# Weights of the first blocks and normalised tokens issued by ScalarE, list scatters spaced anew, in a cross-attention and mixture-of-experts kernel

## The chip, the cores and the metric

The kernel runs on one core of one Trainium2 chip. The metric is the device time of one launch in microseconds (us). An engine is named by its role: TensorE (PE, matrix products; PEld are its weight loads), VectorE (DVE), ScalarE (ACT), GpSimd (POOL) and SyncE (SP), which only starts DMAs. ScalarE and SyncE have a hardware DMA queue each; GpSimd starts the indirect DMAs (gathers and scatters), whose rows are picked by indices.

## The reference

Four batches of 1024 tokens of width 256 pass a cross-attention with 16 heads over 77 context rows, and then a layer of 9 experts of which each token uses 2. Cut to what matters:

```python
x = x + xattn(ctx, layernorm(x), ...)      # 16 heads, 77 keys for each batch
xf = layernorm(x)                          # (4096, 256)
probs = softmax(xf @ Wr)                   # 9 experts
topk_w, topk_idx = top_k(probs, 2)
cw = scatter(topk_w / sum(topk_w))         # (4096, 9), two entries in a row
gate = silu(einsum('th,ehi->tei', xf, Wg)) # 256 -> 704
hidden = gate * einsum('th,ehi->tei', xf, Wu)
x = x + einsum('tei,eih,te->th', hidden, Wd, cw)
```

## The kernel before

**Two halves.** The first half is the attention. It works on 32 sub-blocks of 128 tokens, 4 of which make a group (8 groups, `NS = 4`, `NG = 8`). The second half is the experts. A token's two (expert, token, weight) entries are written into a list in DRAM, `list_d`, which has a stretch for every expert. Blocks of 128 or 256 places of that list are then worked one after another: a gather of the entries (`ids`), a gather of the normalised tokens (`yin`, from `y_d` in DRAM), a turn (`px`, `xT`), the products with Wg and Wu (`hidden_pair`, tiles `pg`, `sl`, `hid`), the product with Wd (`down`, tiles `po`, `co`), and a scattered add into the output (`adding`).

**The order is written out by hand.** Each engine runs its instructions in the order in which the Python code emits them, and a queue's DMAs go out in that order, too. An instruction that waits holds up all that stand behind it on its engine.

**The attention loop** (lines 1667 to 1765) runs 33 steps. Step i does for sub-block i the scores in three parts (`scores`, L295, TensorE, then the row maximum on VectorE; `exponentials`, L312, ScalarE). For sub-block i - 1 it scales the attention weights (`attention_weights`, L334), turns them in blocks of 32 on VectorE (`weights_turn`, L352) and sends them to DRAM as `a_d`; `weights_back` (L360) reads them back as `aT` in four DMAs, with the parts in the other order. For sub-block i - 3 (`LAG = 3`) it multiplies `aT` with the values (`values`, L372, tile `po`). The tile `anT`, from which `a_d` is written, exists once, so the next turn on VectorE waits until `a_d` has been read out. TensorE's order in a step is: the three parts of the scores, then the values. The values of sub-block 29 come in step 32, behind the turn of block 0's tokens; those of sub-blocks 30 and 31 come inside block 0, behind its first and its fourth chunk (`in_first`, L1788).

**Routing**, once for each group, is spread over the steps: `residual`, `root`, `logits`, `exponential`, `normalised` (L977: ScalarE makes the normalised tokens `y`, four activations, and SP writes them to `y_d`), `choices`, `ranks`, `places`. `places` puts eight scatters of the group on the list `pending`; `scatter` (L1065) sends one of them, behind an instruction that is named to it, so that they go out one by one.

For groups 0 to 5 the write of `y` is put off to the end of the step (`written`, L1756), behind `weights_back`; for groups 6 and 7 it is issued at once.

**Early blocks.** Blocks 0 to 5 (`EARLY = 6`) hold places that are known to be full from groups 0 to 3 alone (`G_EARLY = 4`), so their gathers wait for the 32 scatters of these groups only. `next_place` (L1647) is called twice in a step. It sends a scatter, or, once the 32 are out and `first_fetch` (L1658) has run (end of step 26), the next of the first gathers. `first_fetch` also prepares the weights of blocks 0 and 1 in parts: `load` (L1360) is a generator with three parts (one DMA for Wg, three for Wu, two for Wd) in front of which the expert's number is read into a register of the issuing engine. One part goes out at the end of a step (L1752), so block 0's weights go in steps 27, 28 and 29; what is left, block 1's weights, goes out behind the loop (L1766).

**Blocks.** `hidden_pair` (L1437) makes a block's hidden rows in six chunks of columns. After each chunk come `pump` (L1574), which emits up to 12 steps of the work that is left over (routing of groups 6 and 7, then the tables of the later blocks), and in blocks 0 and 2 to 5 some scatters: four behind each of chunks 1 to 4 of block 0, two behind each of chunks 0 to 4 of blocks 2 to 5. When the late tables reach a marked point (`PLACES`), `pump` sends all that is pending. `fetch` (L1597) runs at the head of each block and starts weights, gathers of entries (`tokens`) and gathers of tokens (`inputs`) some blocks ahead. The gather of block 6's entries waits for all 64 scatters; `tokens` (L1388) sends what is still pending in front of it.

Of the kernel before, what the change touches and what calls it, by code (L numbers as in the profile page):

```python
# [15 lines left out]
P = 128  # L16
# [5 lines left out]
def kernel(  # L22
# [18 lines left out]
    nc = tc.nc  # L41
# [6 lines left out]
    E, _, FF = wg.shape  # L48
# [4 lines left out]
    NS = TB // P  # L53
    NG = TOK // TB
    GPB = N // TB
    NF = FF // P
    FT = FF - NF * P
# [43 lines left out]
    G_EARLY = NG - 4  # L101
# [193 lines left out]
    def scores(i, k):  # L295

        h, n = banks[k]
        if k == 0:
            nmx[i] = stat.tile([P, H], F32, tag="mx", name=f"mx{i}")
        psc = pscs[k] = ps_sc.tile([P, TB], F32, tag=f"sc{k}", name=f"psc{i}_{k}")  # L300
        w = n * J + (E if h + n == H else 0)
        for c in range(C):
            strips(
                psc[:, :w], turned_query(i, c), g_sb[i // NS // GPB][:, c, h * J : h * J + w],
                start=(c == 0), stop=(c == C - 1),
            )
        return nc.vector.tensor_reduce(  # L307
            nmx[i][:, h : h + n], psc[:, : n * J].rearrange("p (h j) -> p h j", h=n), AX.X,
            ALU.max, negate=True,
        )  # L310
# [597 lines left out]
    for b in range(B):  # L908
        for m in range(2):
            at = 2 * b + m  # L910
# [66 lines left out]
    def normalised(g):  # L977

        y = pools["rpool"].tile([P, NS, D], F32, tag="y", name=f"y{g}", bufs=1)
        r = routed[g]["r"]  # L980
        o = off_mean("fo", g, routed[g]["mv"], r)
        for s in range(NS):
            yield nc.scalar.activation(
                y[:, s, :], xg[g][:, s, :], AF.Identity,
                bias=o[:, s : s + 1], scale=r[:, s : s + 1],
            )
        written.append(
            lambda: nc.sync.dma_start(out=y_d.rearrange("(g p s) d -> g p s d", p=P, s=NS)[g], in_=y)
        )
        if g > NG - 3:  # L990
            written.pop()()
# [73 lines left out]
    def scatter(behind=None):  # L1065

        if not pending:
            return
        place_i, entry, s = pending.pop(0)
        i = nc.gpsimd.indirect_dma_start(  # L1070
            out=list_d[:, :],
            out_offset=bass.IndirectOffsetOnAxis(ap=place_i[:, s : s + 1], axis=0),
            in_=entry.bitcast(I32)[:, s, :], in_offset=None,
            bounds_check=E * LP - 1, oob_is_err=False,
        )
        if behind is not None:
            after(i, [behind], "the lists' places go out one by one")

        apart(i, sent, "other places of the lists")
        apart(i, early_got, "an early block's places are those of earlier groups")  # L1080
        sent.append(i)
# [242 lines left out]
    def weights(j, in_parts=False):  # L1324

        _, i, kind = blocks[j]
        if kind == "quad2":
            wgus[j], downs[j] = quads.pop(i)
            return
        if j == LAST:  # L1330
            w, d = late["w", uppers[j][0]], late["d", uppers[j][0]]
        else:
            w = pools["wpool"].tile([P, C, 2 * FF], F32, tag="wgu", name=f"wgu{j}")
            d = of(wds, next_down[0])
            next_down[0] += 1
        more = uppers.get(j, ()) if j < LAST else ()
        wgus[j] = (w, *(late["w", n] for n in more))
        downs[j] = (d, *(late["d", n] for n in more))
        if kind == "quad":
            quads[i] = wgus[j], downs[j]  # L1340
        at = PARTS[kind] * i
        parts = load(tabs[kind][0][0:1, at : at + 1], w, d)
        if in_parts:
            partly.append(parts)
        else:
            advance(parts)
# [10 lines left out]

        return begin

    def load(number, w, d):  # L1360
        e = nc.values_load(number, engines=[mybir.EngineType.SP], min_val=0, max_val=E - 1)
        wg_v = wg.rearrange("e (c p) f -> e p c f", p=P)[bass.ds(e, 1)].rearrange("o p c f -> (o p) c f")
        wu_v = wu.rearrange("e (c p) f -> e p c f", p=P)[bass.ds(e, 1)].rearrange("o p c f -> (o p) c f")


        nc.sync.dma_start(out=w[:, :, 0:FF], in_=wg_v)
        yield True
        nc.sync.dma_start(out=w[:, :, FF : FF + FT], in_=wu_v[:, :, NF * P :])
        nc.sync.dma_start(out=w[:, :, FF + FT : FF + FB], in_=wu_v[:, :, FA : NF * P])
        nc.sync.dma_start(out=w[:, :, FF + FB :], in_=wu_v[:, :, 0:FA])  # L1370
        yield True
        nc.sync.dma_start(
            out=d[:, 0:NF, :],
            in_=wd[bass.ds(e, 1), 0 : NF * P, :].rearrange("o (f p) d -> p (o f) d", p=P),
        )
        nc.sync.dma_start(
            out=d[64:128, NF, :], in_=wd[bass.ds(e, 1), NF * P : FF, :].rearrange("o p d -> (o p) d")
        )
        yield True
# [57 lines left out]
    def hidden_pair(j, also={}, upcoming=iter(())):  # L1437

        (w,), xT, hid = wgus.pop(j), xTs.pop(j), hids[j % 2]
        for f in range(NF + 1):  # L1440
            pg = mm_tile(f"pg{j}_{f}").rearrange("p (g t) -> p g t", g=2)
            for g, at in enumerate((f * P, UP[f]) if f < NF else (f * P,)):
                for c in range(C):
                    nc.tensor.matmul(  # L1444
                        pg[:, g, :], w[:, c, at : at + P], xT[:, c, :],
                        start=(c == 0), stop=(c == C - 1),
                    )
            sl = pools["spool"].tile([P, TS], F32, tag="sl", name=f"sl{j}_{f}")
            if f < NF:
                nc.scalar.activation(sl, pg[:, 0, :], AF.Silu)  # L1450
                made = nc.vector.tensor_tensor(hid[:, f, :], pg[:, 1, :], sl, ALU.mult)  # L1451
                for _ in range((0, 4)[f > 0] if not j else 2 if j > 1 else 0):
                    scatter(made)
            else:
                nc.scalar.activation(sl[64:128, :], pg[0:64, 0, :], AF.Silu)
                nc.vector.tensor_tensor(
                    hid[64:128, NF, :], pg[64:128, 0, :], sl[64:128, :], ALU.mult
                )
            pump()
            advance(upcoming, 3)  # L1460
            for fn in also.get(f, ()):
                fn()
# [111 lines left out]
    def pump():  # L1574

        if held[0]:
            held[0] -= 1
            return
        for _ in range(STEP if rest else 0):
            got = next(rest[0], None)  # L1580
            if got is None:
                rest.pop(0)
                if not rest:
                    fetch()
                return
            if got is PRODUCT:
                held[0] = HOLD
                return
            if got is PLACES:
                while pending:  # L1590
                    scatter()
                return

    UPPER = [(f"upper{k}", weights_upper(k), LEAD + k) for k in range(1, SETS + 1)]
# [2 lines left out]
    def fetch():  # L1597

        end = known()
        lead_y = LEAD_Y if late else LEAD  # L1600
        for name, fn, lead in (
            ("weights", weights, LEAD), *(UPPER if late else ()),
            ("inputs", inputs, lead_y), ("tokens", tokens, lead_y + 2),
        ):
            if name == "inputs":

                while ahead["tokens"] < min(now[0] + lead_y + 1, end):
                    advance(tokens(ahead["tokens"]))
                    ahead["tokens"] += 1
            while ahead[name] < min(now[0] + lead + 1, end):  # L1610
                got = fn(ahead[name])
                if name in ("inputs", "tokens"):
                    advance(got)
                ahead[name] += 1
# [32 lines left out]
    def next_place(behind):  # L1647

        if first_gathers and len(sent) >= 2 * NS * G_EARLY:
            got = next(first_gathers[0], None)  # L1650
            if got is None:
                first_gathers.pop(0)
                return next_place(behind)
            after(got, [behind], "gathers go out one by one")
        else:
            scatter(behind)
# [10 lines left out]
    for i in range(N_SUB + 1):  # L1667
# [33 lines left out]
            ranks(q - 1)  # L1701
        if now_on:
            if i:
                scores(i, 2)
                exponentials(i, 2)
                queries_logits(i)
            if i + 2 < RIDE:
                query(i + 2)
            if RIDE <= i + FAR < N_SUB:
                query(i + FAR)  # L1710
            if i:
                extra(i, 2)
            if i == END:
                vsides.close()
        else:
            turn(0)
# [136 lines left out]
```

## Time and profile before

| what | value |
|---|---|
| median of 11 runs | 847.27 us (846.0 to 853.17) |
| the profiled execution, time / span | 847.53 us / 845.8 us |
| mean granted TensorE clock | 0.998 |
| attention loop, TensorE's last scores | end at about 320 us |
| block 0's first product to the last product | 332.88 to 837.98 us |
| VectorE, ScalarE, GpSimd busy | 68%, 44%, 36% |
| SP's queue | 166.96 MB, 62.4% of the 16 DMA engines |
| ScalarE's queue | 70 packets, under 0.01 MB |

The span runs from the first to the last instruction. In an order of time, a row gives the start in us, the duration in us, the engine, the line, the operation and its tiles, and in square brackets how long the engine had stood idle before and what released it. `SPq` rows are the issues of SP's DMAs, not the transfers. The list of waits gives, for an engine and what it waited for, the total in us, how often, and the longest. A table by stretches of time gives each engine's busy time and the busy share of the DMA engines (1.0 is all 16 busy).

Around the end of the loop the DMA engines are busy as follows (share, GB/s), by that table: 288 to 292 us 1.05, 353; 296 to 300 us 1.09, 254; 304 to 308 us 0.85, 201; 308 to 312 us 1.04, 366; 320 to 324 us 0.37, 129; 336 to 340 us 0.49, 161; 344 to 348 us 1.06, 370.

### The profile page before, as it was taken

The numbers are of one execution on the slowest core, as the hardware profiler recorded it, in microseconds if no ns is written. First come the engines' busy times: TensorE is split into PE (matmuls) and PEld (weight loads), VectorE is DVE, ScalarE is ACT, GpSimd is POOL, SyncE is SP. The second block draws the span as 40 slices with busy tenths as digits, with TensorE's granted clock in tenths as the row PEclk, the third lists the DMA queues.
The fourth block names the chain that finished last, engine by engine and source line by source line (L and its number), as shares of the span: only waits on it lengthen the run. The fifth ranks groups of instructions, "written<-read, shape, count | busy, mean of one in ns | idle before, by whom it ended". The sixth has DMA issues, their size and how long they took to land. (4 is left out here: it accounts for less than half of the span.)

```text
span 845.8 us, 20860 instructions
## 1 busy us (share of the span) xinstructions
PE 831.3 (98%) x7334; PEld 581.4 (69%) x7334; DVE 579.0 (68%) x1887; ACT 374.4 (44%) x1543; POOL 307.1 (36%) x344
## 2 busy tenths in 40 slices
PE   8999999999999997999999999999999999999996
PEld 6634444445554454788889788788778878877895
DVE  5767779898899986445854585584677566667550
ACT  4778787878878876142222222222222222222221
POOL 3100000123331232577654444544444463453522
PEclk9999999999999999999999999999999999999999
DMA  8028768778578797986785799789779888788421
GB/s 294 5 100 229 207 211 234 226 232 255 180 229 248 218 281 220 330 258 172 206 243 133 207 334 350 188 259 307 209 230 348 265 243 278 209 245 256 115 26 19
DMA packets 129448, 186.04 MB, mean 220 GB/s; under 512 B 26167, under 2 KB 95295, under 8 KB 129216
## 3 DMA queue, kind: packets, MB, share of 16 engines
q1 hardware_dynamic: 111930, 166.96, 62.4%
q0 software_dynamic: 17344, 17.75, 11.8%
q8 instruction: 58, 0.95, 0.5%
q14 instruction: 46, 0.38, 0.1%
q10 hardware_dynamic: 70, 0.00, 0.0%
HBM read 141.08 MB, written 45.00 MB: 220 GB/s over the span
## 5 line engine op out<-in xcount | busy, mean ns | idle before, releaser
L1444 PE MATMUL pg<-xT,wgu 128*128 128x256 f32 x1100 | 243.1, 380 | 0.1
L1444 PEld LDWEIGHTS pg<-xT,wgu 128*128 128x128 f32 x1100 | 208.3, 190 | 30.1 <-issue 1.3
L1560 POOL DMA_INDIRECT out_dram<-co,ids x73 | 116.7, 1599 | 206.6 <-ACT co L1542 131.2
L318 ACT ACTIVATE ex<-psc,mx 128x77 f32<-128x77 f32 x512 | 158.8, 330 | 60.9 <-DVE mx L307 58.5
L1539 PE MATMUL po<-wd,hid 128*128 128x256 f32 (+2 forms) x768 | 173.2, 380 | 0.0
L1539 PEld LDWEIGHTS po<-wd,hid 128*128 128x128 f32 (+2 forms) x768 | 138.7, 183 | 28.6 <-issue 6.2
L143 PE MATMUL po<-u,aT 128*32 128x265 f32 x2560 | 149.5, 387 | 4.4 <-DMA aT<-a_d 4.4
L1417 DVE STREAM_TRANSPOSE xT<-yin 32x128 f32<-32x128 f32 (+1 forms) x528 | 144.7, 274 | 9.0
L1070 POOL DMA_INDIRECT list_d<-line,r_pli x64 | 63.3, 989 | 240.0 <-DVE mx L307 160.5
L1451 DVE TENSOR_TENSOR hid<-pg,sl 128x256 f32<-128x256 f32 x130 | 55.0, 424 | 119.5 <-ACT sl L1450 116.7
L143 PEld LDWEIGHTS po<-u,aT 128*32 128x32 f32 x2560 | 84.6, 110 | 65.8 <-issue 2.9
L1450 ACT ACTIVATE sl<-pg 128x256 f32<-128x256 f32 x130 | 49.8, 384 | 179.0 <-PE pg L1444 169.5
L143 PE MATMUL psc<-g,aT 128*32 128x462 f32 (+1 forms) x1296 | 118.3, 510 | 0.0
L318 ACT ACTIVATION_READ_ACCUMULATOR ex<-psc,mx 128x1 f32 x512 | 107.5, 210 | 0.0
L143 PEld LDWEIGHTS psc<-g,aT 128*32 128x32 f32 x1296 | 42.2, 109 | 64.3 <-issue 51.0
L1542 ACT ACTIVATE co<-po,ids 128x256 f32<-128x256 f32 x66 | 31.2, 474 | 124.6 <-PE po L1539 120.5
L1383 POOL DMA_INDIRECT yin<-y_d,ids x66 | 69.2, 1049 | 34.8 <-issue 17.4
L307 DVE TENSOR_REDUCE mx<-psc 128x6 f32<-128x462 f32 (+1 forms) x96 | 54.3, 565 | 21.6 <-PE psc L143 21.5
L356 DVE STREAM_TRANSPOSE anT<-an 128x1536 f32<-128x1536 f32 x32 | 56.6, 1770 | 4.6 <-DMA a_d<-anT 4.3
L1529 DVE STREAM_TRANSPOSE hid<-hs 32x160 f32<-32x160 f32 (+1 forms) x112 | 39.5, 353 | 1.7
L340 DVE TENSOR_TENSOR an<-ex,rs 128x1024 f32<-128x1024 f32 x32 | 39.2, 1226 | 1.1
L1472 PEld LDWEIGHTS pt<-xT,wgu 128*128 128x128 f32 x308 | 35.1, 192 | 2.1 <-issue 2.0
(378 smaller groups left out, 764.8 us busy)
## 6 DMA issues: line engine op xcount, KB each, us to landing
a_d<-anT SPq DMA_DIRECT2D x32, 768.0 KB
aT<-a_d SPq DMA_DIRECT2D x128, 192.0 KB
wgu<-in_L_ffn_Wg_dram SPq DMA_DIRECT2D x33, 704.0 KB
wd<-in_L_ffn_Wd_dram SPq DMA_DIRECT2D x33, 640.0 KB
wgu<-in_L_ffn_Wu_dram SPq DMA_DIRECT2D x33, 512.0 KB
w_up<-in_L_ffn_Wg_dram SPq DMA_DIRECT2D x12, 704.0 KB
d_up<-in_L_ffn_Wd_dram SPq DMA_DIRECT2D x12, 640.0 KB
w_up<-in_L_ffn_Wu_dram SPq DMA_DIRECT2D x12, 512.0 KB
```

The lines of the kernel that those rows point to most:

```text
L143: nc.tensor.matmul(out[a : a + Q], left(a), right, **kw)
L307: return nc.vector.tensor_reduce(nmx[i][:, h : h + n], psc[:, : n * J].rearrange("p (h j) -> p h j", h=n), AX.X, ALU.max, negate=True,)
L318: nc.scalar.activation(exs[i][:, h + q, :], pscs[k][:, q * J : (q + 1) * J], AF.Exp, bias=nmx[i][:, h + q : h + q + 1], accum_out=sms[i][: ...
L356: made = nc.vector.transpose(turned, an_of[0].rearrange("p (k q t) -> p q k t", q=NQ, t=Q))
L1070: i = nc.gpsimd.indirect_dma_start(out=list_d[:, :], out_offset=bass.IndirectOffsetOnAxis(ap=place_i[:, s : s + 1], axis=0), in_=entry.bit ...
L1383: return nc.gpsimd.indirect_dma_start(out=dst, out_offset=None, in_=src, in_offset=bass.IndirectOffsetOnAxis(ap=offsets, axis=0), **kw,)
L1417: yield nc.vector.transpose(xT[q : q + Q].rearrange("p c (h t) -> p h c t", t=P)[:, :nh, :, a : a + Q], of(yins, j)[a : a + Q].rearrange(" ...
L1444: nc.tensor.matmul(pg[:, g, :], w[:, c, at : at + P], xT[:, c, :], start=(c == 0), stop=(c == C - 1),)
L1450: nc.scalar.activation(sl, pg[:, 0, :], AF.Silu)
L1451: made = nc.vector.tensor_tensor(hid[:, f, :], pg[:, 1, :], sl, ALU.mult)
L1539: nc.tensor.matmul(po[rows, :D], hid[:, f, at], d[:, f, :], start=(f == 0), stop=(f == NF))
L1560: i = nc.gpsimd.indirect_dma_start(out=out_r, out_offset=bass.IndirectOffsetOnAxis(ap=ids[j][:, h, word : word + 1], axis=0), in_=cos[j][: ...
```

## The change

It has four parts.

1. `normalised` issues the write of `y` on ScalarE's queue in place of SP's, for all eight groups, at the same places of the program.
2. `load` takes the queue as an argument. The weights that go out in parts, those of blocks 0 and 1, are issued on ScalarE's queue, and the expert's number is read into ScalarE's register. All other weights stay on SP.
3. From step 24 on, `next_place` is called a third time in each step, behind the third part of the scores.
4. In the blocks, one scatter goes out behind each of the six chunks of blocks 0 to 3, in place of the four and two of before, and the marked point in `pump` sends nothing any more. So that the gather of block 6's entries (and with it the flush in front of it) doesn't come before that, `fetch` holds `tokens` to the early blocks until block 4.

```diff
@@ normalised
-            lambda: nc.sync.dma_start(out=y_d.rearrange("(g p s) d -> g p s d", p=P, s=NS)[g], in_=y)
+            lambda: nc.scalar.dma_start(out=y_d.rearrange("(g p s) d -> g p s d", p=P, s=NS)[g], in_=y)
@@ weights
-        parts = load(tabs[kind][0][0:1, at : at + 1], w, d)
+        parts = load(tabs[kind][0][0:1, at : at + 1], w, d, nc.scalar if in_parts else nc.sync)
@@ load
-    def load(number, w, d):
-        e = nc.values_load(number, engines=[mybir.EngineType.SP], min_val=0, max_val=E - 1)
+    def load(number, w, d, queue=nc.sync):
+        e = nc.values_load(number, engines=[queue.engine], min_val=0, max_val=E - 1)
...
-        nc.sync.dma_start(out=w[:, :, 0:FF], in_=wg_v)
+        queue.dma_start(out=w[:, :, 0:FF], in_=wg_v)
         yield True
-        nc.sync.dma_start(out=w[:, :, FF : FF + FT], in_=wu_v[:, :, NF * P :])
-        nc.sync.dma_start(out=w[:, :, FF + FT : FF + FB], in_=wu_v[:, :, FA : NF * P])
-        nc.sync.dma_start(out=w[:, :, FF + FB :], in_=wu_v[:, :, 0:FA])
+        queue.dma_start(out=w[:, :, FF : FF + FT], in_=wu_v[:, :, NF * P :])
+        queue.dma_start(out=w[:, :, FF + FT : FF + FB], in_=wu_v[:, :, FA : NF * P])
+        queue.dma_start(out=w[:, :, FF + FB :], in_=wu_v[:, :, 0:FA])
         yield True
...
@@ hidden_pair
                 made = nc.vector.tensor_tensor(hid[:, f, :], pg[:, 1, :], sl, ALU.mult)
-                for _ in range((0, 4)[f > 0] if not j else 2 if j > 1 else 0):
-                    scatter(made)
             else:
                 nc.scalar.activation(sl[64:128, :], pg[0:64, 0, :], AF.Silu)
-                nc.vector.tensor_tensor(
+                made = nc.vector.tensor_tensor(
                     hid[64:128, NF, :], pg[64:128, 0, :], sl[64:128, :], ALU.mult
                 )
+            if j < EARLY - 2:
+                scatter(made)
@@ pump
             if got is PLACES:
-                while pending:
-                    scatter()
                 return
@@ fetch
+            if name == "tokens" and now[0] < EARLY - 2:
+                end = min(end, EARLY)
             while ahead[name] < min(now[0] + lead + 1, end):
@@ attention loop
-                scores(i, 2)
+                third = scores(i, 2)
+                if i >= (G_EARLY + 2) * NS:
+                    next_place(third)
```

More of the change, by code (lines that the diff above doesn't have):

```diff
@@ L1358, in weights_upper @@
         return begin
-    def load(number, w, d):
-        e = nc.values_load(number, engines=[mybir.EngineType.SP], min_val=0, max_val=E - 1)
+    def load(number, w, d, queue=nc.sync):
+        e = nc.values_load(number, engines=[queue.engine], min_val=0, max_val=E - 1)
         wg_v = wg.rearrange("e (c p) f -> e p c f", p=P)[bass.ds(e, 1)].rearrange("o p c f -> (o p) c f")
         wu_v = wu.rearrange("e (c p) f -> e p c f", p=P)[bass.ds(e, 1)].rearrange("o p c f -> (o p) c f")
-        nc.sync.dma_start(out=w[:, :, 0:FF], in_=wg_v)
+        queue.dma_start(out=w[:, :, 0:FF], in_=wg_v)
         yield True
-        nc.sync.dma_start(out=w[:, :, FF : FF + FT], in_=wu_v[:, :, NF * P :])
-        nc.sync.dma_start(out=w[:, :, FF + FT : FF + FB], in_=wu_v[:, :, FA : NF * P])
-        nc.sync.dma_start(out=w[:, :, FF + FB :], in_=wu_v[:, :, 0:FA])
+        queue.dma_start(out=w[:, :, FF : FF + FT], in_=wu_v[:, :, NF * P :])
+        queue.dma_start(out=w[:, :, FF + FT : FF + FB], in_=wu_v[:, :, FA : NF * P])
+        queue.dma_start(out=w[:, :, FF + FB :], in_=wu_v[:, :, 0:FA])
         yield True
-        nc.sync.dma_start(
+        queue.dma_start(
             out=d[:, 0:NF, :],
@@ L1375, in load @@
         )
-        nc.sync.dma_start(
+        queue.dma_start(
             out=d[64:128, NF, :], in_=wd[bass.ds(e, 1), NF * P : FF, :].rearrange("o p d -> (o p) d")
```

## The prediction

> **What bounds the kernel now.** I read the page's busy times first, then TensorE's waits, then TensorE and the SP queue in order of time around the places where TensorE stands still.
>
> ```profile
> PE 831.3 (98%) x7334; PEld 581.4 (69%) x7334; DVE 579.0 (68%) x1887; ACT 374.4 (44%) x1543; POOL 307.1 (36%) x344
> PE po L143 <- DMA aT<-a_d: 4.4, 3, 2.4
> ```
>
> TensorE (PE) is busy for 831.3 of 845.8 us, so a change can only gain what lies in the other 14.5 us. In order of time, 7.8 us of these follow its last matmul (it ends at 837.98 of 845.8: scaling, scattered adds), about 2 us are at the start, 0.15 us is at 370, and 4.4 us are three waits for `aT`, the turned attention weights that go out to DRAM (`a_d`) and come back. The change touches neither end. **Its whole possible gain is these 4.4 us**, 0.52%.
>
> ```profile
> 320.57 4.69 PE L143 MATMUL po<-u,aT 128*32 128x265 f32 x80 [0.56 <-DMA aT<-a_d]
> ...
> 328.27 4.69 PE L143 MATMUL po<-u,aT 128*32 128x265 f32 x80 [2.42 <-DMA aT<-a_d]
> ...
> 336.29 4.69 PE L143 MATMUL po<-u,aT 128*32 128x265 f32 x80 [1.42 <-DMA aT<-a_d]
> 340.91 5.45 PE L1444 MATMUL pg<-xT,wgu 128*128 128x256 f32 x24
> 346.29 4.69 PE L143 MATMUL po<-u,aT 128*32 128x265 f32 x80
> ```
>
> The `po` rows are the value products of sub-blocks 28 to 31 (the last one sits inside block 0). The first three waited 0.56, 2.42 and 1.42 us; the fourth, at 346.29, did not. Why aT is late is seen on the SP queue:
>
> ```profile
> 284.61 2.60 SPq L366 DMA_DIRECT2D aT<-a_d  x4
> ...
> 290.67 0.42 SPq L1366 DMA_DIRECT2D wgu<-in_L_ffn_Wg_dram  x1
> 292.36 1.75 SPq L366 DMA_DIRECT2D aT<-a_d  x4
> 296.04 0.34 SPq L357 DMA_DIRECT2D a_d<-anT  x1
> 296.59 1.26 SPq L1368 DMA_DIRECT2D wgu<-in_L_ffn_Wu_dram  x1
> ...
> 303.10 2.61 SPq L366 DMA_DIRECT2D aT<-a_d  x4
> ...
> 330.08 2.09 SPq L366 DMA_DIRECT2D aT<-a_d  x4
> 332.33 0.34 SPq L357 DMA_DIRECT2D a_d<-anT  x1
> 337.86 1.73 SPq L366 DMA_DIRECT2D aT<-a_d  x4
> ...
> 342.36 0.40 SPq L1366 DMA_DIRECT2D wgu<-in_L_ffn_Wg_dram  x1
> ```
>
> Each `aT x4` is issued when the `a_d` before it has landed, so the distance from one aT to the next is one turn of the chain. Before the first weights it was 7.75 us (284.61 to 292.36). Then `wgu` of block 0 goes into the same queue: 10.74 us (to 303.10), 10.09 (to 313.19), 9.42 (to 322.61). Then, with nothing else in the queue, 7.47 (to 330.08) and 7.78 (to 337.86). TensorE takes some 8.9 us for a sub-block, 4.36 of scores and 4.67 of values with a small overlap. The three long turns lose 10.74 + 10.09 + 9.42 - 3 x 8.9 = 3.6 us against it; the last two can't win that back, because behind the loop's last scores TensorE asks for aT sooner (4.69 + 1.99 = 6.7 us after po(29) began).
>
> **The change part by part.**
>
> *Weights of block 0 leave the SP queue* (one issue in step 27, three in step 28, two in step 29). Their bytes stay: 704 + 704 + 704 KB. Off the queue they no longer stand ahead of aT, but they share the DMA engines with it, and these are full there: 1.05, 1.00 and 1.09 busy from 288 to 300 and 1.04, 0.92 and 0.98 from 308 to 320, with a gap only from 300 to 308 (0.83, 0.85). So the order changes more than the sum. Bounds for the start of the last aT, aT(31), now 337.86: nothing gained, 337.9; or three turns at 8.9, or the limit that VectorE sets, which turns weights 30 only behind the maximum of the last scores, at 320.06 + 0.62 = 320.7, and two turns of 7.5 from there: 335.7. I take 337.3, near the upper end, since the engines are full: the weights of step 27 also start 3 us later than now (ScalarE is busy back to back until 293.4) and so meet a_d(27) and aT(27) rather than aT(26).
>
> The Trainium skill, "DMA: Bandwidth & Descriptors", section "Issuing engines are not separate DMA queues", speaks against any gain: queues of different engines run on the same 16 DMA engines, and a second issuer saves issue time only. By that rule aT gains nothing and the sum below would be 847.7. Its section "Queues, rings and completion order" says that a DMA engine goes round the queues it has work for, packet by packet, which would let aT pass the weights and make the sum 844.3; no row here shows two full hardware queues side by side.
>
> *ScalarE issues instead.* The trace shows no such DMA on it but three tiny ones at the start (0.52, 0.22, 0.27 us). From SP's rows: the read of the expert's number took 1.07 us at 289.0 and 1.29 at 340.6 (0.27 on repeats), register work 0.2, an issue 0.37 to 0.43 at a pitch of 0.57. Step 27: 1.07 + 0.2 + 0.1 + 0.42 = 1.8 us. Step 28: 3 x 0.57 + 0.43 for y = 2.1. ScalarE has waits of only 0.32 + 0.33 us there, so the exponentials of sub-block 29 end 3.9 - 0.65 = 3.3 us later, at 310.1 in place of 306.8. TensorE wants that bank for scores(30, 2) at 306.87 + 2 x 1.45 = 309.8: a new wait of 0.3 us, between none (if issuing overlaps the queued activations) and 1.5 (if Wu's first issue takes 1.26 as on SP). All of it lies in front of the 0.56 us wait, which it shortens: nothing. Were that wait gone, it would cost the 0.3.
>
> *y.* Groups 0 to 4 cost ScalarE 0.43 us each, hidden by its distance to TensorE (step 25's exponentials end at 271.5, the next scores need the last bank at about 275). Group 6's is taken together with the next point. Group 7's is not hidden:
>
> ```profile
> 363.76 1.28 ACT L1450 ACT_TABLE_LOAD   x1
> 365.05 0.66 ACT L1450 ACTIVATE sl<-pg 128x256 f32<-128x256 f32 x2
> ...
> 369.37 0.59 ACT L1433 COPY xT<-px 128x512 f32<-128x512 f32 x1
> ```
>
> ScalarE finishes y(7) at 363.74, loads its table, and the two `sl` behind it are already late; xT of block 2 (369.37) ends 0.05 us before TensorE starts block 2 at 370.01, after standing still for 0.15. An issue of 0.34 to 0.43 us plus its hand-over, say **0.45**, goes through to TensorE in full; bounds 0 and 0.6.
>
> *Weights of block 1 move forward.* Now SP issues all six from 342.36, behind aT(31). From ScalarE they follow y(6), which ends at 335.2: y(6)'s write, 1.3 + 0.2 for the number, six issues at 0.57 make 335.2 to 340.6. On ScalarE that delays only block 0's first `sl` (336.5 now); its bank is wanted again at 346.29, so it is hidden with 4 us to spare. On the DMA side it isn't: 2112 KB of weights and 512 KB of y meet aT(31). Undisturbed, aT takes from issue to its product 7.38, 5.66 and 6.21 us (the three waits), so now aT(31) is there at 343.5 to 345.3, and 346.29 covers it by 1.0 to 2.8 us. 768 KB of aT take 2.1 to 3.5 us by themselves (366 and 227 GB/s, the rates of 308 to 312 and 328 to 338); sharing half the engines adds as much again. Bounds: 0 (the weights fit into 336 to 340, where DMA is 0.49 busy) and 3.5 (half rate all through; even wholly behind the 2.1 MB of weights it would be 2.16/0.369 = 5.9). I take 2.6.
>
> **The sum** is read at po(31), where all three waits, new and old, are paid: 337.3 + 5.7 + 2.6 = 345.6 instead of 346.29, -0.7; +0.45 for y(7): **-0.25 us**. The waits of 0.56 and most of 2.42 go; some 1.5 before po(30) stays, because chain and products are both short there; a new wait of about 2 us stands before po(31). Profile: 845.8 - 0.25 span, 847.53 - 0.25 = 847.3 as a run. The median of the runs shown is 847.27, 0.26 below the profiled one: 847.0.
>
> *Scatters and gathers.* GpSimd's work is not on the path. With three in a sub-block, group 3's eight places are out in step 26, not 27, and the first gathers start one step sooner; their tokens, now issued from 303.61, are first used at 325.19 (`px`), so that gains nothing. The list's tail decides when block 6's places can be read: now the last scatter ends at 404.3, the read is at 409.13, the tokens are issued until 414.6, and `px` of block 6 is at 425.65. Later: 9 + 8 + 8 = 25 pending places, at most 24 go out behind chunks, 1 to 3 remain for the flush in front of that same read, at 1.29 each, behind block 2's adds. That is -1 to +3 us, so tokens by 417.6 + 4.7 (median landing) = 422.3: 3 us of cover. Past that each us would stop TensorE at block 6. The rule that holds tokens of block 6 back until block 4 changes nothing: they go out in block 4 now, too. SP has no compute behind it; without y and weights its next wait is block 2's weights, needed 20 us later.
>
> **Rivals.**
> 1. *The weights of block 1 crowd out aT(31)* (slower). One mechanism, at 336 to 346. If nothing was gained before (issue 337.9), aT needs 7.4 as aT(28) did beside the weights, and half rate adds 3.5: 348.8, +2.5; with 0.45 to 0.6 more: **+3.1, 850.4**. It is slower by over 0.3% once aT(31) is ready after 348.4 (346.29 + 2.54 - 0.45). For it: full DMA engines, and that 2.6 MB now come before the last turn, not behind it. Against: half-empty DMA from 336 to 340.
> 2. *The chain comes free* (faster). Two queues let aT pass. Then aT(31) goes at 335.7 and, if the weights don't touch it, is there at 341.4, while TensorE without any wait comes at 346.29 - 4.4 = 341.9. Of these 4.4, VectorE's date for weights 30 leaves a wait: 320.7 + 7.5 + 5.7 = 333.9 for po(30), where TensorE comes at 336.29 - 4.4 = 331.9, less what the chain gains if a_d(30) needn't queue behind aT(29), 0.5 to 2.0; I take 1.0. So -4.4 + 1.0 + 0.45: **-3.0, 844.3**. For it: turns of 7.5 to 7.8 as soon as the queue is clear. Against: DMA busy 1.0.
> 3. *Nothing but the issuer changes*: all waits stay, y(7) adds 0.45: **847.7**. It lies within the forecast's own range.
>
> **How the numbers follow.** A measurement tells about 0.3%, 2.5 us, from no change; the runs shown lie mostly between 846.0 and 849.2. Forecast with rival 3: 0.53. Rival 2: 0.24. Rival 1, with ScalarE's issues costing more than SP's: 0.23. The likeliest case spans 845.4 to 848.4 by itself; with both others taken in until a tenth is left on each side, 844.3 to 849.9.
>
> **What would show it.** Right: aT(29) waits under 1 us, a wait before po(31) of 1 to 3 us, the waits for aT summing to 3 to 4.5 us, 0.4 more before block 2, SP's turns from 292 to 322 at 9 to 10 us. Rival 2: the sum of aT waits under 1.5 us. Rival 1: a wait before po(31) over 4 us. The forecast is wrong in kind if TensorE waits for ScalarE's exponentials by more than 1.5 us around 310, or for block 6's tokens at all.

## The result, and the profile after

The changed kernel takes **858.16 us** (median of 8 runs, 857.04 to 859.97); the kernel before, run beside it, 847.12 us (31 runs). The ratio is 1.013, its 95% interval 1.0117 to 1.0143: about 11 us slower, where the prediction had 847.0 us and a range that ended at 849.9. The profiled execution has a span of 857.2 us, 11.4 more than before.

First the head of the page of the changed kernel: span, TensorE's busy time, and the clock that TensorE was granted, in tenths, in 40 slices.

```profile
span 857.2 us, 20881 instructions
PE 835.3 (97%) x7334; PEld 594.3 (69%) x7334; DVE 578.1 (67%) x1887; ACT 373.3 (44%) x1543; POOL 306.1 (36%) x344
PEclk9999999999999999899999999999999999999998
```

TensorE is busy for 835.3 us where it was 831.3. It has the same 7334 products, so 4 us of the loss are products that run longer; the rest is waiting. Its waits (us in total, times, longest) name one cause, as before:

```profile
PE po L143 <- DMA aT<-a_d: 11.7, 5, 7.1
```

11.7 in place of 4.4. In order of time (start, duration, ..., wait in front of it and what ended it), the value products of sub-blocks 27 to 31 of the changed kernel:

```profile
311.81 4.69 PE L143 MATMUL po<-u,aT 128*32 128x265 f32 x80 [0.57 <-DMA aT<-a_d]
...
321.94 4.69 PE L143 MATMUL po<-u,aT 128*32 128x265 f32 x80 [0.97 <-DMA aT<-a_d]
...
330.14 6.05 PE L143 MATMUL po<-u,aT 128*32 128x265 f32 x80 [2.93 <-DMA aT<-a_d]
...
338.27 4.69 PE L143 MATMUL po<-u,aT 128*32 128x265 f32 x80 [0.15 <-DMA aT<-a_d]
342.88 5.45 PE L1444 MATMUL pg<-xT,wgu 128*128 128x256 f32 x24
355.39 7.06 PE L143 MATMUL po<-u,aT 128*32 128x265 f32 x80 [7.06 <-DMA aT<-a_d]
```

Two things are to be seen. The first four waits sum to 4.6 us, as much as the 4.4 before: nothing was won there. And po(31), which did not wait before, waits 7.06 us. The durations show the rest: po(29) and po(31) take 6.05 and 7.06 us where all others take 4.69. In the windows of 2 us around po(31) (busy time, products, granted clock, DMA share, GB/s) the clock stands at half:

```profile
350.00:352.00 2.00, 0.00 (x0) 1.00 1.11 231
352.00:354.00 2.00, 0.00 (x0) 0.86 1.06 290
354.00:356.00 2.00, 0.60 (x8) 0.50 0.71 257
356.00:358.00 2.00, 2.00 (x24) 0.50 0.96 206
...
360.00:362.00 2.00, 2.00 (x39) 0.93 0.98 338
```

**The sum of the loss:** waits 11.7 - 4.4 = 7.3; slow products (6.05 - 4.69) + (7.06 - 4.69) = 3.7; together 11.0 of the 11.4 us of span.

Why aT(31) comes late shows on the two issuing queues and in the DMA traffic. SP's queue in the changed kernel:

```profile
298.86 0.34 SPq L357 DMA_DIRECT2D a_d<-anT  x1
305.15 2.54 SPq L366 DMA_DIRECT2D aT<-a_d  x4
...
332.52 1.73 SPq L366 DMA_DIRECT2D aT<-a_d  x4
334.41 0.34 SPq L357 DMA_DIRECT2D a_d<-anT  x1
341.40 4.84 SPq L366 DMA_DIRECT2D aT<-a_d  x4
```

aT(31) is issued at 341.40 (before: 337.86), and its four issues are stretched over 4.84 us. The list of SP's waits from 333 to 350 us says what two of them waited for:

```profile
SPq L366 <- DMA y_d<-y: 6.6, 1, 6.6
SPq L366 <- DMA wgu<-in_L_ffn_Wu_dram: 2.4, 1, 2.4
```

In the same stretch of the kernel before, aT's issues wait for nothing but a_d:

```profile
SPq L366 <- DMA a_d<-anT: 5.1, 1, 5.1
```

By the semaphore updates in the changed kernel's trace, a_d(31) had landed at 339.96 and the write of y(6) at 341.32. So the first issue of aT(31) waited 1.4 us longer than its own data asked, for y(6), and the third waited 2.4 us for a part of block 1's Wu. aT reads neither of the two; the wait is for a completion semaphore that they hold, which is explained below with the run e18. On ScalarE, y(6) and then block 1's weights go out just ahead of it:

```profile
335.57 2.06 ACT L983 ACTIVATE y<-x,fo,r_r 128x256 f32<-128x256 f32 x4
337.66 0.34 ACTq L988 DMA_DIRECT2D y_d<-y  x1
338.81 0.39 ACTq L1366 DMA_DIRECT2D wgu<-in_L_ffn_Wg_dram  x1
...
341.03 0.38 ACTq L1372 DMA_DIRECT2D wd<-in_L_ffn_Wd_dram  x1
345.25 0.53 ACTq L1376 DMA_DIRECT2D wd<-in_L_ffn_Wd_dram  x1
345.81 1.28 ACT L1450 ACT_TABLE_LOAD   x1 [8.18 <-DMA wgu<-in_L_ffn_Wu_dram]
```

The last issue comes 3.8 us behind the fifth, and ScalarE computes nothing for 8.18 us, from the end of y to its table load; that will matter below. The DMA queues (packets, MB, share of the 16 engines; q10 is ScalarE's, q1 SP's) from 341.5 to 344.9, when two quarters of aT(31) had been issued:

```profile
q10 hardware_dynamic: 893, 1.04, 90.9%
q8 instruction: 1, 0.02, 1.7%
```

and from 345 to 354:

```profile
q1 hardware_dynamic: 769, 1.44, 65.9%
q10 hardware_dynamic: 813, 0.86, 42.9%
```

For 3.4 us SP's queue moves no packet. The first one of aT(31) starts at 345.0, 3.6 us behind its issue; in the kernel before it is 0.9 us. So aT(31) does not share with the weights that were issued ahead of it at first, it stands behind them. Then it shares with their rest, with `out_dram` and with block 2's Wg.

### The profile page after: what moved, and what is told of

Its sections match the earlier page's. It is cut to its first block, busy times and chain, and to the rows that moved or that the text cites. A ratio compares the mean times of both kernels' runs of the same rounds, so it can differ in the third digit from the quotient of the medians.

```text
span 857.2 us, 20881 instructions
## 1 busy us (share of the span) xinstructions
PE 835.3 (97%) x7334; PEld 594.3 (69%) x7334; DVE 578.1 (67%) x1887; ACT 373.3 (44%) x1543; POOL 306.1 (36%) x344
## 5 line engine op out<-in xcount | busy, mean ns | idle before, releaser
L143 PE MATMUL po<-u,aT 128*32 128x265 f32 x2560 | 153.6, 394 | 11.7 <-DMA aT<-a_d 11.7
L143 PEld LDWEIGHTS po<-u,aT 128*32 128x32 f32 x2560 | 93.1, 111 | 68.6 <-DVE bn_f L393 7.4
L143 PEld LDWEIGHTS psc<-g,aT 128*32 128x32 f32 x1296 | 46.5, 109 | 60.2 <-issue 48.9
```

The source lines that it names most:

```text
L143: nc.tensor.matmul(out[a : a + Q], left(a), right, **kw)
```

## The experiments

The main theory before the runs, **place**: what costs is that block 1's 2.1 MB stand ahead of aT(31). Its rivals: **chain** (block 0's issues on ScalarE make the chain of a_d and aT late), **issuer** (issues hold up ScalarE), **scatter** (the list's new places).

Chips turned out to differ: the kernel before took 847 us on the chips of the first four runs and of the last two, and 870 to 872 us on three others. So ratios are compared within a group, and waits with care.

**The parts undone one by one (847 us).** In the call of the loader and in the write of y, by turns:

```diff
-        parts = load(..., nc.scalar if in_parts else nc.sync)
+        parts = load(..., nc.scalar if in_parts and j == 0 else nc.sync)   # e1
+        parts = load(..., w, d)                                            # e2, e4
-            lambda: nc.scalar.dma_start(out=y_d..., in_=y)
+            lambda: nc.sync.dma_start(out=y_d..., in_=y)                   # e3, e4
```

Block 1's weights back on SyncE:

> The changed kernel with one thing undone: block 1's weights are issued by SyncE again, block 0's stay on ScalarE. Place theory: block 1's first 2.1 MB stand in front of aT(31), and that is what the changed kernel pays; with them behind, the 7.06 us wait before po(31) and the 2.37 us that po(31) took above 4.69 are gone, 9.4 us together: 848 to 850 us. The other waits (0.57, 0.97, 2.93) and the slow po(29) stay. Chain theory: the loss comes from block 0's issues on ScalarE, which make a_d(27) wait for aT(26) and push the chain 2 to 3.5 us back: no more than half comes back, above 853 us. Scatter theory: nothing comes back, 857 to 859 us.

All weights back on SyncE:

> The changed kernel with both blocks' weights on SyncE, so that the last y blocks from ScalarE and the new places of scatters and tokens are what is left. Place theory and chain theory alike: no weights ahead of aT(31), a_d(27) no longer behind aT(26), the waits of the kernel before (4.4 us) return: 846.5 to 848.5 us. Scatter theory: 857 to 859 us. If the y blocks on ScalarE cost something of their own, the time lies over that of the run with y on SyncE too.

y back on SyncE, weights on ScalarE:

> The changed kernel with the last y blocks issued by SyncE again, weights of blocks 0 and 1 still on ScalarE. Place theory: block 1's weights still go ahead of aT(31): 855 to 858.5 us, with a wait before po(31) of 5 us or more. ScalarE theory (the y issues hold up its activations, or the chain): 848 to 853 us.

y and all weights on SyncE, only scatters, gathers and tokens as changed:

> Only the new places of list scatters, of gathers and of normalised tokens; y blocks and all weights on SyncE as before. Place theory: the last scatter is 15 us later than before but nothing waits for it, so 846.5 to 848 us, no change. Scatter theory: 855 us or more.

| kernel | weights 0 / 1 / y from | median us | ratio to before (95%) | wait before po(31) |
|---|---|---|---|---|
| changed | ACT / ACT / ACT | 858.16 | 1.013 (1.0117 to 1.0143) | 7.06 |
| e3 | ACT / ACT / SP | 855.14 | 1.0087 (1.0071 to 1.0104) | 3.26 |
| e1 | ACT / SP / ACT | 849.37 | 1.0035 (1.0023 to 1.0048) | none |
| e2 | SP / SP / ACT | 848.45 | 1.0028 (1.0012 to 1.0044) | none |
| e4 | SP / SP / SP | 848.48 | 1.0027 (1.0016 to 1.0039) | none |

From the changed kernel to e1 the ratio falls by 0.0095, 8 us: moving **block 1's weights** to ScalarE is nearly the whole loss. TensorE in e1 no longer waits at po(31), and the products run at 4.69:

```profile
337.93 4.69 PE L143 MATMUL po<-u,aT 128*32 128x265 f32 x80 [2.04 <-DMA aT<-a_d]
342.55 5.45 PE L1444 MATMUL pg<-xT,wgu 128*128 128x256 f32 x24
347.93 4.69 PE L143 MATMUL po<-u,aT 128*32 128x265 f32 x80
```

e2 against e4: y from ScalarE costs nothing that can be measured by itself. e3: with block 1's weights on ScalarE too, it does. y(6)'s 512 KB then stand in the same queue just ahead of the weights; without them the wait before po(31) is 3.26 instead of 7.06 us and the median 3 us lower. (e3's profiled execution is its slowest, 859.15 us: TensorE waits 3.1 us for a first weight near the start, which the profiles of e1, e2 and e4 don't have. Its waits before po(31) can be read all the same.) What ends aT(31)'s wait on SP's queue in e3 is a weight:

```profile
SPq L366 <- DMA wgu<-in_L_ffn_Wg_dram: 7.4, 1, 7.4
```

a_d(31) lands at 344.70 there, block 1's Wg at 348.31, and aT(31) goes out at 348.38: 3.6 us of waiting for a semaphore that Wg holds, about as long as TensorE then waits. e1 against e2: block 0's weights on ScalarE may cost 0.9 us; the intervals overlap. e4: the scatters' new places cost 0.27%, 2.3 us, where none was expected, and the profile does not show it (its profiled execution, the fastest of seven, has a span of 845.3 us). The scatter theory as the main cause falls; this small part of it stays open.

**Where block 1's weights stand, still from ScalarE.** e13 issues only Wg (704 KB) behind the loop and the rest behind the fifth chunk of block 0; e5 issues all six there.

```diff
     for parts in partly:
-        advance(parts)
+        advance(parts, 1)          # e13 only; e5 drops the loop
-    in_first = {..., 4: [lambda: turn(1)]}
+    in_first = {..., 4: [lambda: [advance(parts) for parts in partly], lambda: turn(1)]}
```

> The changed kernel with block 1's weights still on ScalarE, but issued behind the fifth chunk of block 0 instead of behind the loop. Place theory: it is the order against aT(31) that costs, not the issuer, so the wait before po(31) goes as in the run with block 1's weights on SyncE: 848 to 850 us, the waits before po(28) to po(30) stay at about 4.5 us. If the issuer counts (six issues between ScalarE's activations inside block 0): above 852 us, with gaps of TensorE inside blocks 0 and 1.

> The changed kernel once more, as the measure for the three runs beside it: the last four runs fell on a chip where the kernel before takes 869.85 us instead of 847, with TensorE waiting for xT in blocks 1 to 3, so they can't be set beside the first four. Where the kernel before takes about 847 us: 856 to 860 us, wait before po(31) 6 us or more. Where it takes about 870 us, the wait for aT(31) lies beside a stall that is there anyway: no more than 5 us slower than the kernel before.

> Block 1's weights still from ScalarE, but behind the fifth chunk of block 0. Place theory: no wait of more than 1 us before po(31) and 8 to 10 us less than the changed kernel on the same chip, where the kernel before takes about 847 us. If the issuer counts, no more than 4 us less.

> The changed kernel with only block 1's Wg (704 KB) issued ahead of aT(31) from ScalarE, its Wu and Wd behind the fifth chunk of block 0. aT(31) then shares no completion semaphore with block 1's weights. If the bytes ahead cost (transfers start in the order of issue over both queues): the 1.4 MB that are gone from the front take 3.8 us at 0.37 MB per us, so the wait before po(31) falls from 7.06 to about 3 us, 851 to 854 us where the kernel before takes 847. If the shared semaphores cost: no wait before po(31), 848 to 850 us. If the issuer costs: 856 us or more.

> Block 1's weights from ScalarE, behind the fifth chunk of block 0 (on the two chips where the kernel before takes 870 us this was no different from it). Where the kernel before takes 847 us, place theory: no wait over 1 us before po(31), 848 to 851 us; block 2's weights now stand ahead of block 1's, so a wait of block 1's first products for weights may cost 1 to 2 us of this. If the issuer counts: above 853 us.

> Only block 1's Wg ahead of aT(31), once more and with more rounds: before, on a chip where the kernel before takes 872 us, the wait before po(31) was 1.05 us and the time 867.5 us, ratio 0.9946 with 0.998 as its upper end. Place theory: the same wait of about 1 us on any chip; where the kernel before takes 847 us that is 849 to 851 us, no gain, since what the other chips gain lies in their own stall behind po(31). If the gain holds on another such chip: ratio 0.993 to 0.998 again; if it was chance: 0.999 or more.

> All of block 1's weights behind the fifth chunk of block 0, beside it. No wait before po(31) in any case. Where the kernel before takes 847 us: 848 to 851 us. Where it takes about 870 us: ratio 0.996 to 1.0.

| run | kernel | before us | median us | ratio (95%) | wait before po(31) | wait for xT of block 1 |
|---|---|---|---|---|---|---|
| e9 | changed | 871.87 | 870.69 | 0.9982 (0.9959 to 1.0004) | 6.33 | none |
| e13 | Wg ahead | 872.23 | 867.52 | 0.9946 (0.9912 to 0.998) | 1.05 | 3.82 |
| e5 | all behind | 869.85 | 869.17 | 0.9989 (0.9972 to 1.0007) | none | 7.9 |
| e10 | all behind | 871.87 | 869.19 | 0.9993 (0.9973 to 1.0013) | none | 7.1 |
| e14 | all behind | 872.23 | 870.27 | 0.9975 (0.9948 to 1.0003) | none | 7.8 |
| e17 | Wg ahead | 847.31 | 858.91 | 1.0136 (1.0115 to 1.0157) | 0.20 | 2.98, and 1.64 for Wu |
| e18 | all behind | 847.31 | 859.20 | 1.0144 (1.0127 to 1.0161) | none | 7.22 |

The wait before po(31) follows the bytes ahead: some 7 us with 2.1 MB, 0.2 to 1.05 with 0.7 MB, none with none. So the place counts, on every chip; whether by the bytes alone is taken up below. But the theory's number for the time did not hold: e18 was to take 848 to 851 us and takes 859.2. The time went one step on. ScalarE in e18:

```profile
355.82 0.38 ACT L1450 ACTIVATE sl<-pg 128x256 f32<-128x256 f32 x1 [6.16 <-PE pg L1444]
356.61 0.38 ACTq L1366 DMA_DIRECT2D wgu<-in_L_ffn_Wg_dram  x1
...
358.38 0.69 ACTq L1370 DMA_DIRECT2D wgu<-in_L_ffn_Wu_dram  x1
360.87 0.38 ACTq L1372 DMA_DIRECT2D wd<-in_L_ffn_Wd_dram  x1
363.11 0.52 ACTq L1376 DMA_DIRECT2D wd<-in_L_ffn_Wd_dram  x1
363.67 0.59 ACT L1433 COPY xT<-px 128x512 f32<-128x512 f32 x1 [7.46 <-DMA wgu<-in_L_ffn_Wu_dram]
```

The six issues take 7 us, because the last two wait at the head of ScalarE's queue, and xT of block 1 stands behind them. TensorE then:

```profile
364.31 3.78 PE L1444 MATMUL pg<-xT,wgu 128*128 128x256 f32 x8 [7.22 <-ACT xT L1433]
```

7.22 us of waiting, and eight products in 3.78 us where they take 1.99 at full clock. What the issues wait for stands in the trace, with the instructions: the DMAs of SyncE's and ScalarE's queues draw on the same eight completion semaphores, and these issues go out only when the last transfer that held their semaphore has landed. In e18 the two issues of block 1's Wd wait for its own Wg and Wu, issued 4.3 and 5.9 us earlier: Wg lands at 360.85 and the first goes out at 360.87, a part of Wu lands at 363.09 and the second goes out at 363.11. In the changed kernel the last Wd waits for Wg in the same way, which is the gap from 341.03 to 345.25 above. There it is covered by the wait for aT(31); with that gone, it is the wait. **So the issuer theory holds as well as the place theory, and the two prices lie on top of each other**: about 9 us each, paid once. e1, e2 and e4, which take block 1's weights off ScalarE and put them behind aT(31), avoid both.

e13 was to tell bytes from shared semaphores, since with Wg alone ahead aT(31) shares none with block 1's weights: bytes alone were to leave 3 us of waiting, semaphores alone none. It left 1.05, and e17 0.20, between the two and nearer to none. Part of what the bytes cost is hidden by the time that TensorE needs to get to po(31), so the way of the data says more. From the landing of a_d(31) to that of aT(31)'s last quarter it is 6.3 us in the kernel before and in e1 (y(6) alone ahead), 8.4 in e17 (y(6) and Wg) and 15.2 in the changed kernel (y(6) and all 2.1 MB). If each 0.7 MB costs the 2.1 us that Wg cost, the 2.1 MB make 6.3 of the 8.9 us (an estimate); the issues that semaphores held for 1.4 and 2.4 us may make the rest. By another sum the bytes would be enough: between the issue of aT(31) and po(31), 341.4 to 355.4, ScalarE's queue moved 1.97 MB and SP's 1.81 MB, of which 0.79 are aT; the other 3.0 MB at the prediction's 0.369 MB per us take 8.1 us, and the way from issue to product is 6.6 to 8.3 us longer than the undisturbed 5.7 to 7.4. How the loss divides between bytes and semaphores stays open: no run kept the weights ahead and gave aT(31) semaphores of its own.

On the 870-us chips the change makes no difference. There another stall lies in the same place. In the kernel before with only block 0's weights moved (e7), ScalarE stands idle until 364.33, and the profile names only "remote" for what ended it:

```profile
364.33 0.39 ACT L1450 ACTIVATE sl<-pg 128x256 f32<-128x256 f32 x1 [14.81 <-remote]
```

and TensorE pays for it behind po(31):

```profile
365.25 3.78 PE L1444 MATMUL pg<-xT,wgu 128*128 128x256 f32 x8 [7.06 <-ACT xT L1433]
```

In e9, the changed kernel there, TensorE stands in front of po(31) instead, and next before block 2 (4.5 us). The wait is put down to `bn_f`, as the releaser that came last by the profile; aT(31), issued from 348.04 to 353.03, is what po(31) reads:

```profile
361.48 6.94 PE L143 MATMUL po<-u,aT 128*32 128x265 f32 x80 [6.33 <-DVE bn_f L393]
```

One stall takes the place of the other. What makes those chips slower stays open, and so does whether e13's small gain there is more than chance: on an 847-us chip the same kernel loses 1.4%.

**Keeping TensorE's clock up.** 48 products, whose result nothing uses, go in front of the last value products of the changed kernel:

```diff
+        keep = ps_sc.tile([P, TB], F32, tag="sc1", name="keep")
+        for _ in range(48):
+            nc.tensor.matmul(keep[:, :P], ident, ones, start=True, stop=True)
```

> The changed kernel with 48 products of the identity with ones (128x128), whose result is used nowhere, put into TensorE's queue ahead of the last value products. They take some 3 us of the 7.06 us that TensorE stands still there. Clock theory: po(31) and what follows are slow (7.06 us in place of 4.69) because TensorE stood still; with a short idle time only, po(31) falls to about 4.7 to 5 us: 855.5 to 856.5 us, 2 us less than the changed kernel. Load theory (the products are slow since DMA fills their operands, or the clock follows something else): po(31) stays at about 7 us: 858 us or more.

> The changed kernel with 48 unused products in front of the last value products. Clock theory: with TensorE idle for under 4.5 us instead of 7, po(31) takes 4.7 to 5.3 us instead of 7.06 and the time is 1 to 2.5 us below the changed kernel's. Load theory: po(31) takes about 7 us and the time is the same or longer.

> The changed kernel with 48 unused products in front of the last value products; on the slow chips po(31) took 4.69 us behind them, against 6.94 us without. Where the kernel before takes 847 us, clock theory: po(31) takes 4.7 to 5.3 us, 855.5 to 857 us. Otherwise 858 us or more.

All three ran where the kernel before takes 870 to 872 us. Medians 872.41, 873.04 and 874.32 us, ratios 1.0025, 1.0032 and 1.0043, each interval just above 1; the changed kernel itself, beside e11, 870.69. TensorE in e11 (the numbering of lines is one further on):

```profile
354.46 10.88 PE L1787 MATMUL keep<-ones,ident 128*128 128x128 f32 x96
365.27 4.69 PE L144 MATMUL po<-u,aT 128*32 128x265 f32 x80
```

po(31) takes 4.69 us where the changed kernel on the same chip (e9, above) takes 6.94, and the granted clock is 1.00 from 350 to 370 us. So the slow products come from TensorE standing still and not from the load on the DMA engines: in the kernel before, po(31) took 4.69 us at a DMA share of 1.06. But the time did not fall. The 48 products appear as 96 instructions and take 10.88 us, not the 3 expected, and run past the wait of 6.3 they were to fill. A shorter filler was not tried.

**Block 0's weights in the kernel before.** Two edits of the kernel before: e7 issues block 0's weights from ScalarE and changes nothing else; e8 moves block 0's Wd behind aT(31) on SyncE.

```diff
-        elif partly and i < N_SUB - 1 and advance(partly[0], 1):
-            partly.pop(0)
+        elif partly and i < N_SUB - 3:      # e8
+            advance(partly[0], 1)
```

> The kernel before with one thing changed: block 0's weights are issued by ScalarE, everything else (y, block 1's weights, scatters, tokens) as before. Chain theory: a_d(27) waits for aT(26) by the shared completion semaphore as in the changed kernel, so the waits before po(28) to po(30) are about 4.5 us, as there, with the slow po(29): 847.5 to 849 us. If issuing block 0's weights elsewhere frees the chain, the waits fall below 4 us: 844.5 to 846.5 us.

> The kernel before with block 0's Wd (704 KB) moved from step 29 of the loop to behind the loop, behind aT(31) in SyncE's queue. If bytes in front of aT make the chain late, the turns of aT(28) to aT(30) get shorter and the waits before po(29) and po(30) fall from 3.8 us to under 2: 844.5 to 846 us. Wd has some 8 us until block 0's down products ask for it; if that is too short, a new wait of theirs eats the gain: 847 us or more.

> The kernel before with block 0's Wd issued behind aT(31) instead of in step 29. On the slow chip the waits for aT were 1.8 us, with no kernel before to set them against. If bytes in front of aT make the chain late: waits of at most 2.5 us instead of 4.4 and 1 to 2 us less than the kernel before, 845 to 846.5 us. If the down products of block 0 then wait for Wd: 847 us or more.

> The kernel before with block 0's Wd behind aT(31). Where the kernel before takes 847 us: if fewer bytes in front of aT shorten the waits, 2.5 us of them or less and 845 to 846.5 us; if the chain is bound by its own turn, waits of 4 us and 847 us as before.

Inconclusive, all on chips where the kernel before takes 870 to 872 us: e7 has a ratio of 1.0013 (0.998 to 1.0045); e8's kernel 0.9999 (0.9971 to 1.0027), 0.9994 (0.9962 to 1.0027) and 0.9974 (0.9944 to 1.0004). The waits for aT were 2.8 us in e7 and 1.8, 1.8 and 3.0 us with Wd later, but there is no profile of the kernel before on such a chip to set beside them. No version was found that beats the kernel before where that takes 847 us; on the other chips only e13 lay below it, by 0.5%.

## Why the prediction was wrong, point by point

- **The bound on the gain (4.4 us of waits for aT)** was read rightly; none of it came. The same waits sum to 4.6 us.
- **"Block 0's weights leave the SP queue"**: aT(31)'s issue was put at 337.3, with 337.9 as the late end; it came at 341.40. The step reckoned with weights out of the way of aT at best, and with no change at worst, and had no bound below nothing. But the chain became later: a_d(27) went out at 298.86 instead of 296.04, because on the shared semaphores it now waited for aT(26) to land, and the turns to aT(28) and aT(31) took 10.7 and 8.9 us. In e2, with all weights on SyncE, aT(31) goes at 337.84, in e1 at 339.75. So block 0's weights account for about 2 us of the delay (one profile each). The other 1.65 us are not a later a_d(31), which lands at 339.69 in e1 and at 339.96 in the changed kernel; there aT(31) waits until 341.32 for the semaphore of y(6).
- **"Weights of block 1 move forward"** is the term that failed: taken at 2.6, bounds 0 and 3.5, it measured 8.3. In the prediction's sum, 337.3 + 5.7 + 2.6 = 345.6 became 341.4 + 5.7 + 8.3 = 355.4 at po(31); TensorE waited 7.06 us for it and lost 2.37 more to slow products. The place was right, and it is rival 1's mechanism; that rival's price, 850.4, was too low for the same reasons. First, both halved the rate where the trace shows no packet of aT at all for 3.4 us. The prediction had worked out 5.9 us for "wholly behind" and set it aside; that was the better bound. Second, the cover of 1.0 to 2.8 us was counted from the old issue at 337.86, and the issue came 3.5 us later. Third, no step let an issue of aT wait for another queue's transfer; two of the four did, for 1.4 and 2.4 us.
- **"That is hidden with 4 us to spare"** (ScalarE's six issues, 335.2 to 340.6): the first five end at 341.4, the sixth waits until 345.25, so ScalarE is held for 8.2 us. No price was put on an issue that waits for a completion. It is hidden only by the loss above; e18 shows what it costs without.
- **TensorE's clock** was in no step. Every wait was priced at its own length, and the two longest cost 3.7 us more. The trace of before gave no warning: its longest wait, 2.42 us, has 4.69 behind it.
- **y(7), +0.45**: nothing. In the changed kernel ScalarE issues it beside the table load that comes anyway:

```profile
375.24 1.28 ACT L1450 ACT_TABLE_LOAD   x1
375.25 0.35 ACTq L988 DMA_DIRECT2D y_d<-y  x1
```

- **Scatters and gathers**: the end of the last scatter was put at 403.3 to 407.3; it comes at 419.2 in the changed kernel, of which the loss explains 11; the read of block 6's places is at 422.68, its tokens end at 430.7, and `px` of block 6 is at 437.07. TensorE waits for none of it, as predicted. The 0.27% of e4 was not.
- **The two rules cited.** The Trainium skill, "DMA: Bandwidth & Descriptors", section "Issuing engines are not separate DMA queues", had a second issuer save issue time only, and its sum was 847.7: aT indeed gained nothing, but here the second issuer lost. Its section "Queues, rings and completion order", by which an engine goes round its queues packet by packet, gave 844.3; no row bears that out between 341.5 and 344.9, where 893 packets of ScalarE's queue go and none of SP's, though from 345 to 354 both run. The measurement decides.

## What to carry to other kernels

Before a transfer is moved to an earlier place or a second queue, list every small, urgent transfer that will be issued behind it on any queue, and price it as standing behind all those bytes, not as sharing with them; look as well whether its own issues draw completion semaphores that those transfers still hold (here 2.1 MB and two held issues, 7 us together). An issue on a computing engine costs its slot only while its completion semaphore is free: look in the program at which earlier DMA holds it, and at what is queued behind the issue. And undo parts in pairs: here undoing the place alone gained nothing, because a second stall of the same length lay beneath it.

## What was not expected of the hardware

- A stop of 2.9 to 7.1 us halves TensorE's granted clock (0.50) and the next products run at half speed for some us: 6.05 and 7.06 us for 4.69. At 2.2 us it can go either way: e2's po(29) took 4.69 behind 2.20 us, e4's 6.37 behind 2.23. In front of each stop before po(29) stand only the four short `px` products (0.65 us), so that from the end of po(28) it is 2.8 us in e2 and e4 and 3.5 in the changed kernel.
- The Trainium skill, "TensorE: Matmul & The Clock Gate", section "Part 1: The HAM clock gate", gives about 3.4 us of idle before the clock is halved; the runs here show it after waits of 2.23 and 2.93 us, or 2.8 and 3.5 us with `px` counted in. The wait in e4 is shorter than that either way.
- Issuing from ScalarE is cheap when nothing is waited for: 0.35 to 0.5 us, beside a table load. It is the wait in front that costs: 3.8 us in the changed kernel, 1.8 and 1.9 us in e18.
- The same two kernels differ by 1.3% where the kernel before takes 847 us, and not measurably on a chip where it takes 872 (e9).
